# Four graph layers in one kernel: when statistics, a root, a short block, a weight product and a few copies are issued

## The chip, the cores and the metric

The kernel runs on one core of a Trainium2 chip. The metric is the device time of one execution in microseconds (us). The kernel before has a median of 2369.26 us over three runs (2368.26 to 2371.22).

A core has five engines with queues of their own, which run side by side and wait for each other by semaphores. The profile calls them PE (matrix products, into PSUM banks of 128 x 512 numbers), PEld (PE's weight load), DVE (element-wise work and statistics), ACT (copies, casts, exp, root), POOL (some element-wise work, and DMAs with computed addresses) and SP (which only issues DMAs).

## The reference, cut to what matters

A graph of 2708 nodes with 512 features passes four layers. Each ends in a layer norm of "x + layer(x)".

```python
deg = jnp.maximum((adj != 0).astype(jnp.float32).sum(-1), 1.0)
# layer 0: dinv = rsqrt(deg); relu(((dinv * (adj + I) * dinv) @ x + x) @ W + b)
x = _layernorm(x + _L0_gnn_ref(x, adj, deg[..., None], L0_gnn_W, L0_gnn_b), axis=-1)
# layer 1: dis = (deg + 1e-8) ** -0.5; ((dis * adj * dis) @ x) @ W.T + b
x = _layernorm(x + _L1_gnn_ref(x, adj, L1_gnn_W, L1_gnn_b), axis=-1)
# layer 2: two attention layers, each:
#   Wh, Ws = split(x @ W); a = softmax(Wh @ Ws.T) * adj; x = leaky_relu(a @ Wh + x)
x = _layernorm(x + _L2_gnn_ref(x, adj, L2_gnn_W_stack), axis=-1)
# layer 3: eight heads, which is adj @ (x @ W) + b
x = _layernorm(x + _L3_gnn_ref(x, adj, L3_gnn_W, L3_gnn_b), axis=-1)
```

The layer norm takes mean and variance over the 512 features of a node, with 1e-5 added to the variance ahead of the root.

## The kernel before, in words

**Tiling.** Nodes are cut into 22 blocks of 128 rows (`NB`), the last of which has only 20. As columns they form six chunks (`CH`): four of 512, one of 384, one of 276, that is of 4, 4, 4, 4, 3 and 3 blocks. As the summed dimension they form six row groups (`GROUPS`) of 4, 4, 4, 4, 3 and 3 blocks.

**Layers 0, 1 and 3** (class `Fast`). `step` goes through (layer, chunk, group). For a group, `prepare` casts adjacency bytes (tile `at`) to a factor `m` and splits the node rows into a high and a low part, `xh` and `xl`. `multiply` then adds `m` times both into the four banks of the chunk, tile `acc`. After the last group `evict` copies the sums into `ht`. While the next chunk is summed, `ends` finishes the one before: in phase 0 `project` multiplies by the weights (tile `mm`) and `combine` adds bias and residual for the first two blocks. In phase 1 the rest follow, and then `finish` calls `layernorm`, which does it for all blocks of the chunk: statistics (`st`, `mv`), the chain of small operations for the root (`rs_v`, `rs_t`, `rs_y`, `y`; one of them on ACT), and a pass per block that writes `o`. `combine` of the 20-row block first adds four partial products into `mm_sb` (`total`). During layer 1, `index` works out for attention which nodes each block takes from (tiles `up`, `rank`, `rest`, `both`, `list`). Its steps wait in a list of jobs and are handed out between the others.

**The two attention layers** (class `Attention`, layers 0 and 1 of their own). Scores of a chunk come from x times a mixed weight (`wst`, tile `mixed`, made by `mix`). For each of the 22 blocks, in the order `js`, `scores` does the products `sp` and ACT copies them to `s`; `greatest` keeps a running maximum (`top`). When the scores of the next chunk have begun, the old chunk's maximum is turned (`tr_top`, `mx`, `wide`, `tr_mx`: the functions `shift_rows` and `shift_columns`), `soften` makes exp and running sums (`sum`) for each block and writes weights to DRAM (`pairs`, by SP). Adjacency being sparse, `fetch` has POOL gather for each block only rows of nodes that occur (`g`). `weigh` multiplies these on PE into `acc`, and `end` scales, adds the residual, applies leaky ReLU, and in layer 1 calls the layer norm (tiles `xr`, `r`) at the chunk's last block.

**Overlap at the seams.** While the last chunk of attention's layer 0 is scored and softened, the generator `second` multiplies the weights of layer 1 (`mix(1)`) and projects. While the last chunk of its layer 1 is, `early` starts layer 3: groups 0 to 3 of its chunks 0, 1 and 2. As PSUM banks are few, the sums of these are copied to SBUF by ACT (tile `begun`) and added again in `evict`.

**What sets the order.** Each engine's instructions run in the order in which the program issues them: the class `Ordered` ties every instruction to the one before on its engine. This is why nearly all lines of the profile bear line 70, that of the helper, and are told apart by tile. Attention has a planner of its own: `advance(us)` moves an estimated clock on by what PE was given, `later(us, what)` puts work off until the clock has got there, and `advance` issues whatever has come due. `weigh` does a product only if the estimated landing of its rows has passed. `until(clock, fill)` takes rows or other layers' work until a time; the variable `done` in `layer` is such a time.

The lines that the change touches: `js` (1696) and `done` (1734) in `layer`, `mix` (1324 to 1346), the end of an attention block (1645 to 1671), `early` (626 to 630), `layernorm` (634), `combine` (976), and in `step` the call of `evict` (1073).

Of the kernel before, what the change touches and what calls it, by code (L numbers as in the profile page):

```python
# [19 lines left out]
P = 128  # L20
N = 2708
D = 512
# [469 lines left out]
class Layer:  # L492


    def __init__(self, number, source, weights, bias):
        self.number, self.source, self.weights, self.bias = number, source, weights, bias
        self.hi, self.lo = [None] * NB, [None] * NB
        self.rows = [None] * NB
        self.acc, self.ht, self.done, self.part = {}, {}, {}, {}
        self.begun = {}  # L500
        self.loaded = set()

# [11 lines left out]
class Fast:  # L514
# [17 lines left out]
    def run(self):  # L532
        kernel, nc = self.k, self.nc
        with ExitStack() as ctx:
            pool = lambda name, bufs, **kw: ctx.enter_context(
                self.tc.tile_pool(name=name, bufs=bufs, reuse_waits="tile", **kw)
            )
            self.pages, self.wides = pool("pages", PAGES), pool("wides", WIDES)
            self.small, self.lists = pool("small_f", 4), pool("lists", 1)
            self.banks = [pool(f"banks{h}", 4, space=PSUM) for h in range(2)]  # L540
            given = [kernel.x_in[bass.ts(i, P), :] for i in range(NB)]
            l0 = Layer(0, given, kernel.w0, kernel.b0)
            l1 = Layer(1, kernel.saved[0], kernel.w1, kernel.b1)
            l3 = Layer(3, kernel.saved[2], kernel.w3, kernel.b3)
            self.attention = attention = Attention(self)
            self.jobs, self.due, self.other, self.beats = [], None, 1, 0
            run = Run(l0, l1)
            for t in range(len(run.seq)):
                self.step(run, t)
            attention.project(attention.layers[0], 0)  # L550
            for g in range(3):
                self.ends(run, g)
                if g == 1:
                    attention.project(attention.layers[0], 1)


            run = Run(l3)
            run.seq = [(l3, k, g) for k in range(TWO) for g in range(4)]
            run.seq += [(l3, k, g) for g in (4, 5) for k in range(2)]
            run.seq += [(l3, k, g) for k in range(2, TWO) for g in (4, 5)]  # L560
            run.seq += [(l3, k, g) for k in range(TWO, len(CH)) for g in range(len(GROUPS))]
            attention.run(self.early(run))
            for j in range(*GROUPS[5]):
                l3.rows[j] = attention.made[j]
            for t in range(4 * TWO, len(run.seq)):
                self.step(run, t)

            ly, k = run.before
            for i, n, ps in self.project(ly, k):
                self.finish(ly, k, [(i, n, self.combine(ly, i, n, ps))])  # L570

    def work(self, engine):

# [24 lines left out]
    def early(self, run):  # L598

        seq = run.seq  # L600
        yield True
        self.load(*seq[0])
        self.load(*seq[1])
        yield True
        self.prepare(*seq[0])
        yield True
        for t in range(4 * TWO):
            ly, k, g = seq[t]
            if t < 2:
                self.attention.need(GROUPS[t + 2][1] - 1)  # L610
            self.load(*seq[t + 2])
            if t == 4:
                self.load_weights(ly)
            if t == 4 * TWO - 1:
                self.attention.need(GROUPS[4][1] - 1)
                for j in range(*GROUPS[4]):
                    ly.rows[j] = self.attention.made[j]
            self.prepare(*seq[t + 1])
            if g == 3:
                ly.begun[k] = []  # L620
            for n, j in enumerate(range(*GROUPS[g])):
                if t == 0:
                    self.multiply(ly, k, g, [j])
                else:
                    self.multiply(ly, k, g, ds=[n])
                self.attention.advance(2 * cost(CH[k][1]))
                if g == 3:
                    b = self.page(f"begun{k}_{n}")
                    self.nc.scalar.copy(b[:, : CH[k][1]], ly.acc[k][n][:, : CH[k][1]])
                    ly.begun[k].append(b)  # L630
                yield True


    def layernorm(self, rows):

        nc, small = self.nc, self.small
        m = len(rows)
        mv = small.tile([P, DC, 2], FP, tag="mv", name="mv")
        if any(n < P for _, _, n in rows):
            nc.vector.memset(mv, 1.0)  # L640
        for q, (r, _, n) in enumerate(rows):
            st = small.tile([P, 6], FP, tag="st", name="st")
            nc.vector.bn_stats(st[:n], r[:n])
            nc.vector.bn_aggr(mv[:n, q, :], st[:n])
        y = small.tile([P, DC], FP, tag="y", name="y")[:, :m]
        self.rsqrt(y, mv[:, :m, 1], LN_EPS)
        for q, (r, o, n) in enumerate(rows):
            nc.vector.tensor_scalar(
                o[:n], r[:n], mv[:n, q, 0:1], y[:n, q : q + 1], ALU.subtract, ALU.mult
            )  # L650
# [322 lines left out]
            x = ly.done["xres", i]  # L973
            self.nc.vector.tensor_add(x[:n], x[:n], ly.bt[:n])

    def combine(self, ly, i, n, ps):

        nc, x = self.nc, ly.done.pop(("xres", i))
        if n <= QW:
            t = self.page(f"mm_sb{ly.number}_{i}")  # L980
            self.total(t[:n], ps, n, D)
            ps = t
        if ly.number == 3:
            nc.vector.tensor_add(x[:n], x[:n], ps[:n])
            return x
        scale = (self.k.rdeg if ly.number == 0 else self.k.dis)[:n, i : i + 1]
        r = self.page(f"r{ly.number}_{i}")
        nc.vector.scalar_tensor_tensor(r[:n], ps[:n], scale, ly.bt[:n], ALU.mult, ALU.add)
        if ly.number == 0:
            nc.vector.scalar_tensor_tensor(x[:n], r[:n], 0.0, x[:n], ALU.max, ALU.add)  # L990
        else:
            nc.vector.tensor_add(x[:n], x[:n], r[:n])
        return x

    def finish(self, ly, k, parts):

        nc, out = self.nc, []
        for i, n, x in parts:
# [1 line left out]
            if n < P and ly.number == 0:  # L1000
                nc.vector.memset(o, 0.0)
            out.append((i, o, n))
        self.layernorm([(x, o, n) for (_, n, x), (_, o, _) in zip(parts, out)])
        for i, o, n in out:
            if ly.number == 3:
                nc.sync.dma_start(self.k.out[i * P : i * P + n, :], o[:n])
# [36 lines left out]
    def step(self, run, t):  # L1043
# [6 lines left out]
        if ly.number == 1 and k == len(CH) - 1 and g in (2, 3, 4):  # L1050
            self.attention.begin(g - 2)
        self.multiply(ly, k, g)
        wide = CH[k][1] == BANK
        if run.before and run.phase in ((1, 3, 4, 5) if wide else (1, 5)):
            self.work("PE")
# [9 lines left out]
        if g == len(GROUPS) - 1:  # L1065
# [4 lines left out]
            while run.before and run.phase < 2:  # L1070
                self.ends(run, run.phase)
                run.phase += 1
            self.evict(ly, k)
            run.before, run.phase = (ly, k), 0
            if ly.number == 1:
                self.jobs.append((k, self.index(k)))
# [2 lines left out]
    def ends(self, run, g):  # L1079
# [3 lines left out]
            run.parts = self.project(ly, k)  # L1083
            run.x = []
        if g in (0, 1):
            some = run.parts[:2] if g == 0 else run.parts[2:]
            run.x += [(i, n, self.combine(ly, i, n, ps)) for i, n, ps in some]
        if g == 1:
            run.o = self.finish(ly, k, run.x)
            if ly.number == 0 and k == len(CH) - 1:  # L1090
# [158 lines left out]
class Chunk:  # L1249


    def __init__(self, ly, k):
# [4 lines left out]
        self.softened = 0  # L1257
        self.fetched, self.rden = [], None
        self.x, self.first = {}, {}

        self.to_weigh = []
        for q, (i, _, _) in enumerate(self.blocks):
# [12 lines left out]
class Attention:  # L1275
# [48 lines left out]
    def mix(self, a):  # L1324
# [5 lines left out]
                nc.sync.dma_start(w[h][c], self.k.w2_t[a, h, bass.ts(c, P), :])  # L1330
        yield True
        ps = [self.bank(1 - a, f"mix{a}_{m}") for m in range(DC)]
        for c in range(DC):
            for m in range(DC):
                nc.tensor.matmul(
                    ps[m], w[1][c][:, bass.ts(m, P)], w[0][c], start=(c == 0), stop=(c == DC - 1)
                )
            self.advance(DC * cost(D))
            yield True
        for m in range(DC):  # L1340
            t = self.page(f"mixed{a}_{m}")
            nc.scalar.copy(t, ps[m])
            if a == 0:
                nc.sync.dma_start(self.mixed[m], t)
            else:
                self.layers[a].mixed.append(t)

    def load_w(self, ly):

# [295 lines left out]
    def end(self, ch, q, acc, x, first):  # L1645
# [3 lines left out]
        )  # L1649
        r = self.page(f"r2_{ch.name}_{q}")  # L1650
        if w < P:
            nc.vector.memset(r, 0.0)
        nc.vector.scalar_tensor_tensor(r[:w], x[:w], SLOPE, x[:w], ALU.mult, ALU.max)
        if ch.ly.number == 1:
            nc.vector.tensor_add(r[:w], r[:w], first[:w])
            ch.ends.append((r, w))
            if q == len(ch.blocks) - 1:
                self.f.layernorm([(r, r, w) for r, w in ch.ends])
                for (i, _, _), (r, _) in zip(ch.blocks, ch.ends):
                    nc.sync.dma_start(self.k.saved[2][i], r)  # L1660
                    self.made[i] = r
            return
        nc.sync.dma_start(self.k.between[i], r)
        ch.ends.append((r, w))
        if q == len(ch.blocks) - 1:
# [3 lines left out]
                    ch.ends, ch.k, 1, f"x2b{ch.k}", self.k.turned[1][ch.k], nc.sync  # L1669
                ),  # L1670
            )


    def run(self, next_layer):
# [15 lines left out]
    def layer(self, ly, chunks, fill):  # L1690
        f = self.f
        self.chunks, self.made = chunks, {}
        for k, ch in enumerate(chunks):
            old = chunks[k - 1] if k else None

            js = [0, 1, NB - 1, *range(2, NB - 1)]
            for n, j in enumerate(js):
                if old and n == 0:
                    self.load_masks(old)
# [31 lines left out]
        self.shift_rows(last)  # L1731
        self.until(self.clock + 3, fill)
        self.shift_columns(last)
        done = self.clock + 2
        while last.softened <= NB:
            self.soften(last)
            done += 1.4
# [106 lines left out]
```

## Time and profile before

| | |
|---|---|
| median of three runs | 2369.26 us |
| the profiled execution's own time | 2338.2 us |
| its span | 2336.5 us |
| mean granted clock of PE | 0.993 |
| PE busy | 2274.8 us, 97% |
| PEld busy | 1292.5 us, 55% |
| DVE busy | 1474.8 us, 63% |
| ACT busy | 662.2 us, 28% |
| POOL busy | 762.3 us, 33% |
| moved by DMA | 463.50 MB, 198 GB/s over the span |

All durations below come from the one profiled execution, whose span is inside its time. In a row of the timeline the columns are the start from the span's start, the duration, engine, line, operation, the written tile and the read ones, shape, count, and in brackets the engine's idle time just ahead and what released it. In the groups, "x" is a number of instructions. In the list of waits the columns are the waiting engine and tile, what ended the wait, the total, how often, and the longest. PE's idle time is what ties the other engines to the total; where another engine is idle, nothing follows from that alone.

### The profile page before, as it was taken

To read this page: it belongs to the slowest core of one execution; us is meant where nothing else is said; L and a number is where in the kernel's file an instruction comes from. 1 tells how busy PE (TensorE), PEld (TensorE's weight loads), DVE (VectorE), ACT (ScalarE), POOL (GpSimd) and SP (SyncE) were. 2 spreads that over 40 slices of the span, in tenths; PEclk is the share of its full clock that TensorE was granted. 3 is DMA by queue.
4 is the path that set the end of the run, shared out by engine and by line. 5 is a ranking of instruction groups with operands and counts; after the bars stand their busy time and mean duration, and the time that the engine had idled before them with its cause. 6 is when DMAs were issued, how large, how long until landed. Compare 5 with 4: busy or idle time off the path is not lost.

```text
span 2336.5 us, 26171 instructions
## 1 busy us (share of the span) xinstructions
PE 2274.8 (97%) x8518; PEld 1292.5 (55%) x8518; DVE 1474.8 (63%) x2831; ACT 662.2 (28%) x1334; POOL 762.3 (33%) x879
## 2 busy tenths in 40 slices
PE   8999999999999999999999999999999999999997
PEld 6677677778644444443456444444443456566585
DVE  6999986786655529657677511228677788724523
ACT  6544353223100113222223200113232334432211
POOL 6645641111000000636375550000636466551000
PEclk9999999999999999999999999999999999999998
DMA  9765652222434404869699996405869799983311
GB/s 343 258 199 169 182 172 86 74 86 70 171 146 167 154 0 143 278 229 311 204 324 350 302 388 232 152 0 163 279 217 314 233 316 329 305 279 96 123 48 43
DMA packets 312440, 463.50 MB, mean 198 GB/s; under 512 B 60162, under 2 KB 189706, under 8 KB 312292
## 3 DMA queue, kind: packets, MB, share of 16 engines
q1 hardware_dynamic: 252276, 240.81, 31.5%
q0 software_dynamic: 60016, 220.92, 27.1%
q8 instruction: 69, 1.13, 0.2%
q14 instruction: 79, 0.65, 0.1%
HBM read 307.75 MB, written 153.85 MB: 198 GB/s over the span
## 4 chain that ended last, share of the span: by engine, by line
PE 84%; DVE 7%; DMA 4%; issue 2%; ACT 1%; POOL 1%; SPq 0%; DVEq 0%; ACTq 0%; POOLq 0%
PE sp L70 32%; PE acc L70 29%; PE mm L70 9%; PE z L70 6%; PE wst L70 6%; DMA pairs<-s 1%; DMA at<-in_adj_t 1%; DVE st L70 1%; DMA at<-mask 1%; ACT m L70 1%; DVE s L70 1%; PE list L70 1%; PE mix L70 0%; POOL bytes L70 0%; PE tr_x2t L70 0%
## 5 line engine op out<-in xcount | busy, mean ns | idle before, releaser
L70 POOL DMA_INDIRECT g<-pairs,givers x510 | 516.2, 1012 | 897.0 <-DMA pairs<-s 537.4
L70 PE MATMUL sp<-xs,wst_sb 128*128 128x512 f32 (+3 forms) x2112 | 797.7, 544 | 0.0
L70 PEld LDWEIGHTS sp<-xs,wst_sb 128*128 128x128 f32 (+1 forms) x2112 | 380.0, 186 | 406.8 <-issue 321.9
L70 PE MATMUL acc<-m,xh 128*128 128x512 f32 (+4 forms) x1584 | 571.4, 382 | 13.6 <-ACT m L70 7.0
L70 PE MATMUL acc<-m,xl 128*128 128x512 f32 (+4 forms) x1584 | 553.2, 367 | 1.5 <-DVE xl L70 1.5
L70 PEld LDWEIGHTS acc<-m,xh 128*128 128x128 f32 (+1 forms) x1584 | 290.3, 189 | 81.4 <-issue 22.3
L70 PEld LDWEIGHTS acc<-m,xl 128*128 128x128 f32 (+1 forms) x1584 | 290.3, 189 | 48.1 <-issue 5.7
L70 ACT COPY s<-sp 128x512 f32<-128x512 f32 (+2 forms) x252 | 133.6, 531 | 482.1 <-PE sp L70 469.5
L70 PE MATMUL acc<-g 128*32 128x512 f32 (+1 forms) x1020 | 260.8, 605 | 0.9 <-DMA g<-pairs,givers 0.5
L70 DVE TENSOR_TENSOR top<-top,s 128x512 f32<-128x512 f32 (+5 forms) x240 | 149.6, 623 | 170.6 <-ACT s L70 169.1
L70 PE MATMUL mm<-w,ht 128*128 128x512 f32 (+1 forms) x528 | 222.6, 593 | 8.1 <-DVE ht L70 8.1
L70 ACT CAST m<-at 128x512 fp32r<-128x512 uint8 (+5 forms) x396 | 199.2, 567 | 80.0 <-DMA at<-mask 63.7
L70 ACT ACTIVATE s<-s 128x512 f32<-128x512 f32 (+3 forms) x264 | 150.7, 580 | 236.6 <-DVE s L70 236.3
L70 DVE TENSOR_TENSOR sum<-sum,s 128x512 f32<-128x512 f32 (+4 forms) x252 | 157.4, 625 | 23.9 <-ACT s L70 23.9
L70 DVE TENSOR_TENSOR s<-s,a 128x512 f32<-128x512 f32 (+3 forms) x264 | 165.9, 628 | 10.2 <-DMA a<-mask 1.2
L70 DVE TENSOR_TENSOR s<-s,shift 128x512 f32<-128x512 f32 (+3 forms) x264 | 162.8, 620 | 6.7 <-ACT shift L70 6.7
L70 PEld LDWEIGHTS mm<-w,ht 128*128 128x128 f32 (+1 forms) x528 | 95.5, 186 | 124.4 <-issue 110.9
L70 PE MATMUL wst<-xt,mixed 128*128 128x512 f32 (+2 forms) x384 | 152.5, 550 | 1.7 <-ACT mixed L70 1.7
L70 PEld LDWEIGHTS acc<-g 128*32 128x32 f32 (+1 forms) x1020 | 75.4, 134 | 136.9 <-issue 115.8
L70 PE MATMUL z<-w,xt 128*128 128x512 f32 (+1 forms) x352 | 151.0, 596 | 0.0
L70 DVE COPY z_sb<-z 128x512 f32<-128x512 f32 (+1 forms) x44 | 30.3, 690 | 179.5 <-PE z L70 176.3
L70 POOL DMA_DIRECT2D x<-o x44 | 26.0, 596 | 358.0 <-DVE o L70 354.2
(167 smaller groups left out, 1657.4 us busy)
## 6 DMA issues: line engine op xcount, KB each, us to landing
pairs<-s SPq DMA_DIRECT2D x378, 128.0 KB
pairs<-z_sb SPq DMA_DIRECT2D x84, 512.0 KB
at<-in_adj_t SPq DMA_DIRECT2D x84, 256.0 KB
xres<-x POOLq DMA_DIRECT2D x44, 256.0 KB, 4.3
x<-o POOLq DMA_DIRECT2D x43, 256.0 KB, 3.1
x<-x SPq DMA_DIRECT2D x37, 256.0 KB
at<-mask SPq DMA_DIRECT2D x32, 256.0 KB
xt<-t SPq DMA_DIRECT2D x32, 256.0 KB
```

The costliest lines, as they stand in the source:

```text
L70: ins = call(*args, **kw)
```

## The change

There are seven edits. First, `layernorm` is split into `means`, `statistics` and `normalize`. `combine` now calls `statistics` as soon as a block is combined, and `finish` calls `normalize` only; the same holds for an attention block's end. Second, in attention's layer 1 the root, the normalizing passes and the saves of a chunk are put off by two planner microseconds. Third, the 20-row block is scored fourth instead of third. Fourth, the weight product of attention's layer 1 is done output part by output part, with each part's copy right behind it. Fifth, in attention's layer 1 the time `done` starts at four instead of two planner microseconds. Sixth, the copies of begun sums are issued ahead of `advance`, and a memset moves from DVE to POOL. Seventh, for chunks with begun sums `evict` is called right after the last product, ahead of the phases of the chunk before.

```diff
@@ early
-                self.attention.advance(2 * cost(CH[k][1]))
                 if g == 3:
                     b = self.page(f"begun{k}_{n}")
                     self.nc.scalar.copy(b[:, : CH[k][1]], ly.acc[k][n][:, : CH[k][1]])
                     ly.begun[k].append(b)
+                self.attention.advance(2 * cost(CH[k][1]))
                 yield True
@@
-    def layernorm(self, rows):
+    def statistics(self, mv, q, r, n):
+        nc = self.nc
+        st = self.small.tile([P, 6], FP, tag="st", name="st")
+        nc.vector.bn_stats(st[:n], r[:n])
+        nc.vector.bn_aggr(mv[:n, q, :], st[:n])
+
+    def means(self, few):
+        mv = self.small.tile([P, DC, 2], FP, tag="mv", name="mv")
+        if few:
+            self.nc.vector.memset(mv, 1.0)
+        return mv
+
+    def normalize(self, mv, rows):
         nc, small = self.nc, self.small
         m = len(rows)
-        mv = small.tile([P, DC, 2], FP, tag="mv", name="mv")
-        if any(n < P for _, _, n in rows):
-            nc.vector.memset(mv, 1.0)
-        for q, (r, _, n) in enumerate(rows):
-            st = small.tile([P, 6], FP, tag="st", name="st")
-            nc.vector.bn_stats(st[:n], r[:n])
-            nc.vector.bn_aggr(mv[:n, q, :], st[:n])
         y = small.tile([P, DC], FP, tag="y", name="y")[:, :m]
@@
-    def combine(self, ly, i, n, ps):
+    def combine(self, ly, k, q, i, n, ps):
+        if q == 0:
+            ly.mv[k] = self.means(any(n < P for _, _, n in blocks_of(k)))
+        x = self.sum(ly, i, n, ps)
+        self.statistics(ly.mv[k], q, x, n)
+        return x
+
+    def sum(self, ly, i, n, ps):
         nc, x = self.nc, ly.done.pop(("xres", i))
@@ finish
-        self.layernorm([(x, o, n) for (_, n, x), (_, o, _) in zip(parts, out)])
+        self.normalize(ly.mv[k], [(x, o, n) for (_, n, x), (_, o, _) in zip(parts, out)])
@@ step
         self.multiply(ly, k, g)
+        if g == len(GROUPS) - 1 and k in ly.begun:
+            self.evict(ly, k)
...
-            self.evict(ly, k)
+            if k in ly.acc:
+                self.evict(ly, k)
@@ ends
-            some = run.parts[:2] if g == 0 else run.parts[2:]
-            run.x += [(i, n, self.combine(ly, i, n, ps)) for i, n, ps in some]
+            for i, n, ps in run.parts[:2] if g == 0 else run.parts[2:]:
+                run.x.append((i, n, self.combine(ly, k, len(run.x), i, n, ps)))
@@ mix
-        for c in range(DC):
-            for m in range(DC):
+        def end(m):
+            t = self.page(f"mixed{a}_{m}")
+            nc.scalar.copy(t, ps[m])
...
+        for e in range(DC):
+            for c, m in [(e, m) for m in range(DC)] if a == 0 else [(c, e) for c in range(DC)]:
                 nc.tensor.matmul(
                     ps[m], w[1][c][:, bass.ts(m, P)], w[0][c], start=(c == 0), stop=(c == DC - 1)
                 )
+            if a == 1:
+                end(e)
             self.advance(DC * cost(D))
             yield True
@@ end of an attention block
         if w < P:
-            nc.vector.memset(r, 0.0)
+            nc.gpsimd.memset(r, 0.0)
         nc.vector.scalar_tensor_tensor(r[:w], x[:w], SLOPE, x[:w], ALU.mult, ALU.max)
         if ch.ly.number == 1:
             nc.vector.tensor_add(r[:w], r[:w], first[:w])
+            if q == 0:
+                ch.mv = self.f.means(ch.cw % P)
+            self.f.statistics(ch.mv, q, r, w)
             ch.ends.append((r, w))
             if q == len(ch.blocks) - 1:
-                self.f.layernorm([(r, r, w) for r, w in ch.ends])
-                for (i, _, _), (r, _) in zip(ch.blocks, ch.ends):
-                    nc.sync.dma_start(self.k.saved[2][i], r)
-                    self.made[i] = r
+                self.later(2, lambda: self.normalize(ch))
             return
...
+    def normalize(self, ch):
+        self.f.normalize(ch.mv, [(r, r, w) for r, w in ch.ends])
+        for (i, _, _), (r, _) in zip(ch.blocks, ch.ends):
+            self.nc.sync.dma_start(self.k.saved[2][i], r)
+            self.made[i] = r
@@ layer
-            js = [0, 1, NB - 1, *range(2, NB - 1)]
+            js = [0, 1, 2, NB - 1, *range(3, NB - 1)]
...
-        done = self.clock + 2
+        done = self.clock + (2 if ly.number == 0 else 4)
```

## The prediction

> **What bounds the kernel.** I read the busy shares first, then the chain, and then TensorE's (PE's) waits, since the groups all carry one line, that of the ordering helper.
>
> The profile's busy row and its chain:
>
> ```profile
> span 2336.5 us, 26171 instructions
> ...
> PE 2274.8 (97%) x8518; PEld 1292.5 (55%) x8518; DVE 1474.8 (63%) x2831; ACT 662.2 (28%) x1334; POOL 762.3 (33%) x879
> ...
> PE 84%; DVE 7%; DMA 4%; issue 2%; ACT 1%; POOL 1%; SPq 0%; DVEq 0%; ACTq 0%; POOLq 0%
> ```
>
> PE is busy 97% of the span and holds 84% of the chain. The change leaves every matrix product in the program, so it can only take from what is left: 2336.5 - 2274.8 = 61.7 us of idle PE, and half-clock stretches. PE's last matmul ends some 17 us before the end, so about 45 us of idle lie inside. PE's waits, total, times and longest:
>
> ```profile
> engine line waited for: us in total, times, longest us
> PE mm L70 <- DVE ht L70: 8.1, 4, 2.6
> PE acc L70 <- ACT m L70: 7.0, 5, 2.9
> PE tr_mx L70 <- DVE wide L70: 4.5, 10, 0.7
> ...
> PE rest L70 <- DVE up L70: 4.1, 1, 4.1
> PE acc L70 <- DVE dg L70: 3.6, 1, 3.6
> PE acc L70 <- ACT begun L70: 2.9, 2, 2.7
> PE tr_top L70 <- DVE top L70: 1.9, 1, 1.9
> PE wst L70 <- ACT mixed L70: 1.7, 1, 1.7
> PE acc L70 <- DVE xl L70: 1.5, 2, 1.2
> ...
> PE acc L70 <- DMA g<-pairs,givers: 0.5, 2, 0.3
> ```
>
> Each part of the change moves work ahead of one of these. Costing it means asking, place by place, what the PE waits for next.
>
> A gap can cost more than itself. PE's timeline around the `begun` wait:
>
> ```profile
> 2119.46 0.39 PE L70 MATMUL acc<-m,xl 128*128 128x512 f32 x1
> 2122.55 0.80 PE L70 MATMUL acc<-m,xh 128*128 128x512 f32 x1 [2.70 <-ACT begun L70]
> 2123.14 0.63 PE L70 MATMUL acc<-m,xl 128*128 128x512 f32 x1
> 2123.57 0.63 PE L70 MATMUL acc<-m,xh 128*128 128x512 f32 x1
> ```
>
> The matmul takes 0.63 instead of 0.39 us, with starts 0.43 apart instead of 0.23; over 2120 to 2125 us the granted clock averages 0.76. Such a stretch is about 3.4 us at half clock and loses 1.7 us. It follows the gaps of 2.9 (ACT m, at 2012), 2.7 (begun), 3.6 (dg) and 4.1 us (rest), but neither the 2.6 us one at 2162 nor one of 2.67 us at 790.
>
> Here a rule is weighed. The Trainium skill, "TensorE: Matmul & The Clock Gate", Part 1, says that the clock halves after an idle window of about 3.4 us, a free-running one. By it a 2.7 us gap would usually cost 2.7 us, and a removal that leaves 1.9 us would bring 0.8. By the row it costs 4.4 and brings 2.5. The row decides where a gap is already there; for a new gap near 2.7 us I take half of the 1.7 us, since such gaps went either way here.
>
> **The change part by part** (us of PE time; the sum is made against the profiled execution's 2338.2 us).
>
> *Statistics per block.* The same instructions (0.66 + 0.18, about 0.8 a block) run as each block is combined, instead of all after the last. That pays where DVE otherwise waits for PE's next product and PE later waits for DVE. Around 652 DVE waits 1.96 us for `mm`; the first of three blocks' statistics fits there, so `up` and `rest` come 0.8 earlier: the gap of 4.1 becomes 3.3. Its half-clock stretch stays. In the same way the gap for `dg` at 309 loses some 0.5 (DVE waits 0.53 before), and the one for `xl` at 344 (1.2) some 0.8. In mid-chunks of layers 0 and 1 PE waits for nothing of this kind: nothing. That is covered by PE's own work; without cover it would cost at most 0.8 a block. The `list` waits (4.2 in all) hang on `both`, which follows PE's own `rest`: unchanged. At the very end blocks 19, 20 and 21 each get their own `memset` of 0.07: 0.15 lost. Sum: **2.1 - 0.15 = 1.95**.
>
> *The 20-row block fourth.* When a chunk's scores start, PE does three blocks and then the four small transposes `tr_mx` of the previous chunk, which need DVE's `wide`. The block just ahead of them is the 20-row one, x8 matmuls in 1.05 us; here at the fifth boundary of layer 0:
>
> ```profile
> 1224.18 0.49 PE L70 MATMUL tr_top<-ident,top 128*128 128x128 f32 x3
> 1224.60 0.66 PE L70 MATMUL sp<-xs,wst_sb 128*20 128x276 f32 x8
> 1226.00 0.52 PE L70 MATMUL tr_mx<-ident,wide 128*128 128x128 f32 x3 [0.74 <-DVE wide L70]
> ```
>
> With a full block there (1.9 us at 276 columns, 3.4 at 512, instead of 0.66 to 1.05), PE comes 1.2 to 2.4 us later and the 0.26 to 0.74 us waits are gone: layer 0 0.26+0.26+0.36+0.57+0.74 = 2.2, layer 1 0.35+0.35+0.36+0.56 = 1.6, **3.8**. Layer 1's last (0.74) is counted below. What goes the other way: the 20-row total (a copy and three adds on DVE, 0.67 + 3 x 0.7 = 2.8 us) now lies after softening has begun, so softening, pair writes (SP) and fetches (POOL) of the old chunk move 2 to 4 us later against PE. Their cover is the 12 to 16 us between a chunk's first fetched rows landing and PE's use of them; without it every us late is a PE us.
>
> *Root put off (attention's layer 1).* The root's chain and the four saves on SP go two planner-us later: on ACT behind the exp of block 20 and a score copy, on SP behind the pair writes of block 19. In mid-chunks the saves are wanted far later: nothing. At 1919 it matters. DVE's root chain there (rs_v 1915.6, four normalizing passes to 1919.1, two `top`) is what `tr_top` waits 1.86 us for. Moved, ACT does the score copy of block 20 first (ends 1915.95), then the table load of 1.28, then the root (1917.4); normalizing ends near 1920.5 instead of 1919.1, `top` twice makes `tr_top` about 1921.8: a gap of 2.7. The 0.74 wait for `tr_mx` goes: 1.86 + 0.74 = 2.6 against 2.7, plus half of 1.7 for the clock: **-1.0** (bounds: +0.5 if the earlier statistics let the whole root start first, -2.5 with the full half-clock stretch and some lateness).
>
> *W2 product by parts.* The PE order is turned round so that output part e is done after four matmuls, and ACT copies it while PE does the next. Before, ACT's four copies (2.03 us) started only at 1304.10:
>
> ```profile
> 1303.76 0.43 ACT L70 ACTIVATE s<-s 128x276 f32<-128x276 f32 x1 [0.76 <-DVE s L70]
> 1304.10 2.03 ACT L70 COPY mixed<-mix 128x512 f32<-128x512 f32 x4
> ```
>
> and `wst` waited for the first. Now only the last part's copy is left at that point, and `wst` needs it at its fourth matmul, 2.6 us in. The copies are ahead of softening's exps on ACT, which come up to 2.2 us later and then have 2 us fewer ahead of them. **1.7**.
>
> *Order after attention's last chunk* (`done` 4 instead of 2 in layer 1). It puts fetched-row products of chunk 4 ahead of layer 3's second row group, so more PE work covers DVE's and ACT's preparation of `m` and `xh`. The waits for `m` at 2012 (2.9 + 0.31 + 0.30), 0.3 nearby, and 1.7 of half clock, some 5.5 in all, go. But the fetched rows are now the late ones: POOL issues one every 1.25 us and each lands some 6 us later, so the six come from 1996.4 to 2003.1, and PE would stand before them for some 4.0 in small waits. **1.5** (bounds -1 to +4; the middle, by the fetch rows of this same stage). DMA is the limit here: its share over 1985 to 2005 is 1.06, over 1965 to 1985 1.04.
>
> *Copies of begun sums ahead of the planner's step.* ACT's copy of the chunk's fourth sum stood behind an `rs_t` that waited for DVE:
>
> ```profile
> 2121.82 0.20 ACT L70 ACTIVATE rs_t<-rs_v 128x3 f32<-128x3 f32 x1 [6.53 <-DVE rs_v L70]
> 2121.93 0.57 ACT L70 COPY begun<-acc 128x512 f32<-128x512 f32 x1
> ```
>
> Now the copy comes first, and the 2.70 gap and its half clock (1.7) go. Next late is the mask page of group 5, queued on SP behind the three saves of that root: it lands about 2127, its fold, high part and `m` take to about 2131, and PE waits some 1.9 there. The `memset` of the last block's result moves to POOL (0.5 less on DVE). 4.4 - 1.9 = **2.5** (bounds 0, if the mask page is later by 2.5; 4.4, if it isn't late).
>
> *Sums of the last chunks taken in early.* For chunks 0 to 2 of layer 3 the four adds into `ht` (0.68 each) are issued ahead of the previous chunk's combination and statistics, so the 2.62 wait at 2162 goes, with 0.27 of slow first matmul. The profile shows DVE at normalizing work just there, from 2156.7 to 2164.1. The statistics and outputs behind them are wanted by nobody on PE. The next sums' banks come free just in time, I allow 0.2. **2.7**.
>
> **Sum:** 1.95 + 3.8 - 1.0 + 1.7 + 1.5 + 2.5 + 2.7 = 13.15 us. The runs shown have a median of 2369.26, 31 above the profiled one; nothing moved here lies in that difference, so I take the same 13.2 us off: **2356 us** (-0.56%). A measurement of this kernel tells 0.2% (4.7 us) from no change.
>
> **The rivals.**
> 1. *As summed*, 0.65: 2350 to 2359, with the unknown terms at their bounds.
> 2. *The end of attention keeps its time*, 0.16. The stage from 1985 to 2165 is bound by fetches and mask pages, and what the last three parts free is waited for at the next page. For it: DMA 0.94 busy over 1985 to 2075. Against: DMA falls to 0.44 by 2115 to 2130, and at 2162 no transfer is named. It leaves 1.95 + 3.8 - 1.0 + 1.7 = 6.5: 2363.
> 3. *The score reordering doesn't do what it says*, 0.12: `wide` is late again behind the moved 20-row total, as DVE is 78% busy over 1568 to 1925, and rival 2 holds too. Against: the total comes after the transposes' inputs in DVE's order. It leaves under 3: 2367, no change to be told.
> 4. *Slower*, 0.07: later softening makes the fetched rows late at ten chunk boundaries. It decides above 13.2 / 10 = 1.3 us per boundary, and shows as slower above 1.8. For it: POOL's fetches wait mostly for pair writes (537 us in the profile's groups), and in the last chunk DVE is 98% busy (19.55 of 20 us, 1945 to 1965). Against: PE waited for fetched rows 0.5 us in the whole run. At 2.5 us each: 2369 - 13 + 25 = 2381.
>
> **How the numbers follow.** The forecast is rival 1's. Faster: 0.65 and nearly all of rival 2, 0.80; same: rival 3 and the rest of 2, 0.13; slower 0.07. The range 2348 to 2366 holds rivals 1 and 2 but for 1's low tail, and part of 3; it leaves out the slower case and about 0.1 besides.
>
> **What would show it.** Right: in the profile after, PE's waits of `tr_mx` for `wide`, of `wst` for `mixed`, of `acc` for `begun` and of `mm` for `ht` near 2162 are missing; `rest` for `up` is near 3.3; PE busy is less only by half-clock time (some 3 us). Also a `tr_top` wait near 2.7, several small `acc` waits for `g` near the last chunk's start, and one of `acc` for `m` of about 2 near group 5. Wrong: `g` waits at each chunk boundary (rival 4), `tr_mx` waits still there (3), or waits for `at` and `g` summing to more than 6 us after 1985 (2).

## The result, and the profile after

The changed kernel has a median of 2357.37 us over seven runs (2350.50 to 2359.66), the kernel before 2368.33 over seven. The ratio is 0.9946, with a 95% interval from 0.9927 to 0.9966: 0.54% faster, where 0.56% was forecast. The total is met. How it comes about is not what was forecast, as the experiments show: the term for the statistics is several times too small, the four edits at the end of attention (root put off, `done`, begun copies, early `evict`) together lose time instead of gaining it, and on one chip the same change gained only a quarter of the sum.

The first profiles can't be laid side by side. That of before took 2338.2 us, 30 less than its own median; that of the changed kernel took 2359.7. The experiments suggest why: the same program has a median of 2341 us on one chip and of 2366 to 2368 on two others. The chips of the first two profiles are not on record. So below, an execution is compared only with one on the same chip.

The busy row of the changed kernel, and PE's waits in it (columns as before):

```profile
span 2357.8 us, 26154 instructions
...
PE 2283.9 (97%) x8518; PEld 1296.6 (55%) x8518; DVE 1478.0 (63%) x2831; ACT 662.4 (28%) x1334; POOL 767.3 (33%) x881
```

```profile
PE acc L70 <- ACT m L70: 8.6, 5, 3.8
PE tr_mx L70 <- DVE wide L70: 6.2, 2, 3.6
PE acc L70 <- ACT begun L70: 5.8, 1, 5.8
PE mm L70 <- DVE ht L70: 5.3, 3, 2.4
...
PE tr_mx L70 <- ACT x2b L70: 3.4, 1, 3.4
...
PE tr_top L70 <- remote: 2.6, 1, 2.6
```

Two lines of before are gone, as forecast: `wst` for `mixed`, and the ten short waits of `tr_mx`. One is there that was not forecast: a wait of 5.8 us for `begun`, twice as long as the one that the change was to remove.

### The profile page after: what moved, and what is told of

It reads as the page before. It is cut to its first block, busy times and chain, and to the rows that moved or that the text cites. A ratio compares the mean times of both kernels' runs of the same rounds, so it can differ in the third digit from the quotient of the medians.

```text
span 2357.8 us, 26154 instructions
## 1 busy us (share of the span) xinstructions
PE 2283.9 (97%) x8518; PEld 1296.6 (55%) x8518; DVE 1478.0 (63%) x2831; ACT 662.4 (28%) x1334; POOL 767.3 (33%) x881
## 3 DMA queue, kind: packets, MB, share of 16 engines
q1 hardware_dynamic: 252276, 240.81, 31.3%
## 5 line engine op out<-in xcount | busy, mean ns | idle before, releaser
L70 DVE TENSOR_TENSOR top<-top,s 128x512 f32<-128x512 f32 (+2 forms) x240 | 149.1, 621 | 150.3 <-ACT s L70 108.9
```

The lines of the kernel that those rows point to most:

```text
L70: ins = call(*args, **kw)
```

## The experiments

Three groups of four kernels, each group on one chip beside the kernel before. The medians are over 5 to 21 runs, those of before over 11 to 51. The ratios are to that kernel, with 95% intervals; they are not always the quotient of the two medians.

| group (median of before) | kernel | median, us | ratio |
|---|---|---|---|
| 1 (2341.21) | before again | 2342.07 | 1.0003 [0.9989, 1.0017] |
| 1 | changed again | 2337.91 | 0.9986 [0.9977, 0.9994] |
| 1 | changed, 20-row block third | 2340.65 | 0.9998 [0.9989, 1.0006] |
| 1 | changed, four end edits undone | 2328.71 | 0.9937 [0.9916, 0.9958] |
| 2 (2366.16) | changed, `done` at 2 | 2355.09 | 0.9950 [0.9933, 0.9968] |
| 2 | changed, root not put off | 2349.39 | 0.9925 [0.9902, 0.9948] |
| 2 | changed, begun copies behind `advance` | 2354.60 | 0.9948 [0.9932, 0.9964] |
| 2 | changed, late `evict` | 2352.93 | 0.9938 [0.9922, 0.9955] |
| 3 (2367.61) | before with the statistics alone | 2356.91 | 0.9959 [0.9943, 0.9976] |
| 3 | changed again | 2354.86 | 0.9949 [0.9931, 0.9967] |
| 3 | changed, four end edits undone | 2346.89 | 0.9920 [0.9899, 0.9940] |
| 3 | before again | 2368.43 | 1.0002 [0.9986, 1.0018] |

### Both kernels once more

No edit.

> The kernel before once more, unchanged: 0% by definition. Two readings of the gap of 30 us between the first profiled execution (2338.2) and the median of its runs (2369.3). Reading 1, that execution was an unusually quick one: this profile lies near 2368 and its PE waits hold some 25 to 30 us more, at places where the changed kernel's profile has them too (DVE and ACT late behind transfers at the ends of attention's layers). Reading 2, profiled executions are quicker: again near 2338 with the same waits.

> The changed kernel once more, unchanged. My sum gives -13 us against the kernel before (ratio 0.9945). If the sum's rows hold, the four waits named in the prediction (wst for mixed, mm for ht near 2162, the short tr_mx waits at chunk boundaries, begun behind rs_t) are missing in this execution too, while the waits of 2.6 to 5.8 us for late transfers in the first profile of it (at 1230, 1930, 1935, 2006, 2052, 2156) change place or size. If those are made by the change itself, they stand at the same places with the same sizes.

Reading 1 of the profile of before is out in this form: here the runs themselves were at 2342, as the first profile had been, and the waits were nearly those of it. The changed kernel gained only 0.14% on this chip (0.06 to 0.23%), some 3 us, where 13.2 were forecast. PE's waits in its profile, span 2333.9 us:

```profile
PE acc L70 <- ACT m L70: 7.9, 6, 3.5
PE acc L70 <- ACT begun L70: 6.3, 1, 6.3
PE mm L70 <- DVE ht L70: 5.9, 3, 2.4
...
PE rest L70 <- DVE up L70: 3.5, 1, 3.5
PE tr_top L70 <- DVE top L70: 2.6, 1, 2.6
PE acc L70 <- DVE dg L70: 2.1, 1, 2.1
PE tr_mx L70 <- DVE wide L70: 1.9, 1, 1.9
PE acc L70 <- DMA g<-pairs,givers: 1.5, 5, 0.5
```

`tr_top` waits 2.6 and fetched rows are waited for five times, as forecast. Of the waits of the first profile that nobody forecast, those near 1230 (3.4) and 1935 (2.6) are not here and the one near 2006 (3.6) is 1.9, so they vary from chip to chip or execution to execution. The one for `begun` is here and in every execution of the changed kernel, so it is the change's own. The one for `m` at group 5 was forecast, at 1.9; it is 3.8 in the first profile and 3.5 here.

To see where time is gained and lost, take the start of the same matmul in the two timelines of group 1, before and changed, from front to back: `rest` 669.3 and 665.4; first `tr_top` of attention 872.9 and 870.6; first `wst` of attention's layer 1 1308.7 and 1300.1; its last `tr_top` 1989.2 and 1977.7; first `mm` of layer 3 2147.0 and 2143.3; PE's last 2325.8 and 2317.6. The gain reaches 11.5 us, falls to 3.7 over the end of attention, and grows to 8.3 behind it (this execution of before was 2 us above its median, and the changed one 2 below). With the four end edits undone the same points of the last three are 1980.6, 2135.8 and 2310.6: gains of 8.6, 11.2 and 15.2. Behind that last `tr_top`, the kernel without the edits gains another 6.6 us on the kernel before, and the one with them loses 3.2. The edits, which were to save 5.7 us, cost 9.8 there.

### The four end edits undone

```diff
-                self.later(2, lambda: self.normalize(ch))
+                self.normalize(ch)
...
-        done = self.clock + (2 if ly.number == 0 else 4)
+        done = self.clock + 2
...
-        if g == len(GROUPS) - 1 and k in ly.begun:
-            self.evict(ly, k)
...
+                self.attention.advance(2 * cost(CH[k][1]))
                 if g == 3:
                     b = self.page(f"begun{k}_{n}")
                     self.nc.scalar.copy(b[:, : CH[k][1]], ly.acc[k][n][:, : CH[k][1]])
                     ly.begun[k].append(b)
-                self.attention.advance(2 * cost(CH[k][1]))
```

> The changed kernel with the four edits at attention's end undone (root put off, done at 4, begun copies first, early evict). My sum: these are worth -1.0 + 1.5 + 2.5 + 2.7 = 5.7 us, so this lies 5.7 above the changed kernel and 7.5 below the one before (ratio 0.997). Rival: the end of attention is bound by fetches and mask pages and the four edits bring nothing: ratio near 0.9945, as the changed kernel.

> The changed kernel without the four end edits once more: as where it was measured first, 5 to 9 us quicker than the changed one beside it (ratio to before near 0.993), with no begun wait above 1 us. Rival: the 9 us were that occasion's; then both are the same.

Neither my sum nor its rival: the kernel was 9.2 us quicker than the changed one in group 1, and 8.0 in group 3, by the medians. In group 1 the intervals lie apart; in group 3 they overlap a little. It beats both kernels on both occasions. PE's waits of it in group 1:

```profile
PE mm L70 <- DVE ht L70: 5.3, 4, 2.4
...
PE acc L70 <- ACT begun L70: 0.8, 1, 0.8
PE tr_top L70 <- DVE top L70: 0.7, 1, 0.7
```

Without the end edits, the waits that these were to remove have shrunk all the same: `begun` 2.7 to 0.8, `tr_top` 1.9 to 0.7, and `mm` for `ht` near 2162 (2.6) is 0.3. The statistics per block, which this kernel keeps, are the likely cause; below they are run alone.

The largest wait that the edits brought in their place is seen around 2022. First the timelines of PE, ACT and SP in the changed kernel:

```profile
2022.48 0.39 PE L70 MATMUL acc<-m,xl 128*128 128x512 f32 x1
2029.16 0.79 PE L70 MATMUL acc<-m,xh 128*128 128x512 f32 x1 [6.29 <-ACT begun L70]
2029.75 0.63 PE L70 MATMUL acc<-m,xl 128*128 128x512 f32 x1
```

```profile
2026.45 2.18 ACT L70 CAST m<-at 128x512 fp32r<-128x512 uint8 x4 [5.19 <-DMA at<-mask]
2028.53 0.57 ACT L70 COPY begun<-acc 128x512 f32<-128x512 f32 x1
```

```profile
2011.24 11.39 SPq L70 DMA_DIRECT2D pairs<-s  x24
2022.68 0.49 SPq L70 DMA_DIRECT2D at<-mask  x1
```

And ACT and SP with the four edits undone:

```profile
2021.08 2.18 ACT L70 CAST m<-at 128x512 fp32r<-128x512 uint8 x4 [1.10 <-DMA at<-mask]
2023.17 0.58 ACT L70 COPY begun<-acc 128x512 f32<-128x512 f32 x1
```

```profile
2008.18 9.84 SPq L70 DMA_DIRECT2D pairs<-s  x21
2018.12 0.38 SPq L70 DMA_DIRECT2D at<-mask  x1
```

On ACT the begun copy stands behind four casts, which wait for a mask page. SP issues that page behind pair writes, three for each block that softening has finished: 24 of them in the changed kernel, 21 without the edits. The page goes out at 2022.68 instead of 2018.12, the copy ends at 2029.1 instead of 2023.8, and the bank that PE wants next is free only then. PE then runs 6.8 us at half clock (0.76 granted on the mean of 2022 to 2036).

Not all of this is loss. Without the edits PE stands a little earlier, and has its half clock there (0.76 over 2008 to 2022, where the changed kernel has 1.00):

```profile
2011.11 0.50 PE L70 MATMUL acc<-m,xh 128*128 128x512 f32 x1 [3.12 <-ACT m L70]
```

So the waits behind the last `tr_top` have to be set against each other. With half-clock losses they sum to 19.0 us in the changed kernel and 8.8 without the edits. The difference of 10.2 is: `begun` 5.5 more; `m` at group 5 2.7 more, and 1.7 for the half clock behind it; `tr_mx` 1.9 more; fetched rows 1.3 more; `m` near 2011 2.6 less, and 0.3 less for `mm`. The half clock at `begun` and that at 2011 cancel.

### The four, one at a time

Each kernel has one of the four pieces of the diff above undone.

> The changed kernel with the root of attention's layer 1 not put off. The recorded step gives the putting off -1.0 us: tr_top's wait falls from 2.6 back to 0.7, as it is without all four end edits (the earlier statistics alone shorten it from 1.9), and the kernel is 1.9 us quicker than the changed one, or 3.6 with a half-clock stretch less. Rival for the 9 us that the four edits cost: the saves and the pair writes change their order on SP, so that mask pages come late; then the wait of 6.3 us for begun goes in this run.

> The changed kernel with done at 2 again in attention's layer 1, the other three end edits kept. New theory after the run without all four: done at 4 lets PE run through the row groups of layer 3 in one stretch (1998.7 to 2022.9), so that it stands before the begun copy, which lies behind casts that wait for a mask page: 6.3 us, and 1.7 of half clock. Then this kernel has no wait of acc for begun above 1 us and is 5 to 8 us quicker than the changed one (ratio to before near 0.996 here). My recorded step has it the other way: 1.5 us slower than the changed kernel.

> The changed kernel with the begun copies behind the planner's step again. PE's order is the same. The recorded step says 2.5 us slower (the wait of 2.7 us at 2120 comes back). If the earlier statistics have already taken most of that wait (0.8 left of 2.7 in the run without the four edits), it is 1 us slower or no different. If the copies' new place makes the wait of 6.3 us at 2029, that wait goes and the kernel is 8 us quicker.

> The changed kernel with the sums of the last layer's first chunks taken in as late as before. The recorded step says 2.7 us slower (mm waits 2.6 for ht near 2162). But without all four end edits that wait is missing too: if the statistics per block alone remove it, no difference (within 0.5 us).

Putting off the root is what makes the wait for `begun`. Of the executions profiled, the seven with the root put off all wait for `begun` around 2030 to 2050: 5.8, 6.3, 6.2 and 8.2 us in the changed kernel and the one with the short block third, 4.7, 6.3 and 3.9 with `done`, the copies and `evict` undone. The three without (this one and twice all four undone) have no such wait there, and none for `begun` above 0.8 anywhere. With the root alone undone, the page stands in SP's order two blocks' writes earlier, 18 of them just ahead of it instead of 24:

```profile
2027.33 8.40 SPq L70 DMA_DIRECT2D pairs<-s  x18
2035.83 0.38 SPq L70 DMA_DIRECT2D at<-mask  x1
```

With `done` at 2 it is 27 with the root put off and 21 without: both times putting off the root adds the writes of two blocks. The kernel's ratio is 0.9925, against 0.9946 and 0.9949 of the changed kernel where that stood beside a kernel before of the same speed: some 5 us, though the intervals overlap. By these numbers the root accounts for about half of what the four edits cost. The wait for `m` at group 5 stays in each of these four kernels (2.5 to 3.9 us), and is 0.8 or less with all four undone: no single undoing removes it, and its cause stays open. My theory for `done` fell: with it undone the wait stayed (4.7), and the time is that of the changed kernel. For the copies and `evict` the times, good to some 4 us, can't tell; the profiles can. With the copies in their old place no begun wait is left near 2150, and with the late `evict` the `mm` wait near 2188 is 0.27 us. Both edits aim at a wait of which the statistics had left little.

### The statistics alone

The kernel before, with `combine` and attention's `end` calling `statistics`, and nothing else.

> The kernel before with the statistics per block alone. The recorded step gives 2 us. New theory, from the runs with the end edits undone: the statistics alone remove what I had put down to the end edits: the mm wait for ht near 2162 (2.6), most of the begun wait (2.7 to 0.8, with its 1.7 of half clock), most of tr_top's wait (1.9 to 0.7), besides rest 4.1 to 3.5 and dg 3.2 to 2: together some 10 us, but 2 to 3 of it go into a wait for m at group 5. So 7 to 8 us below the kernel before (ratio 0.9968), and the ten tr_mx waits (4.5) stay.

0.9959 [0.9943, 0.9976] or 9.7 us, with bounds of 5.7 and 13.5: the 7 to 8 expected lie inside, the 2.0 of the step on record does not. Three of its waits from the end of attention on, in PE's timeline:

```profile
1934.91 0.52 PE L70 MATMUL tr_top<-ident,top 128*128 128x128 f32 x3 [0.60 <-DVE top L70]
...
2151.08 0.50 PE L70 MATMUL acc<-m,xh 128*128 128x512 f32 x1 [1.23 <-ACT begun L70]
...
2190.01 2.41 PE L70 MATMUL mm<-w,ht 128*128 128x512 f32 x5 [0.28 <-DVE ht L70]
```

And in the kernel before on the same chip:

```profile
1937.33 0.52 PE L70 MATMUL tr_top<-ident,top 128*128 128x128 f32 x3 [1.75 <-DVE top L70]
...
2149.25 0.50 PE L70 MATMUL acc<-m,xh 128*128 128x512 f32 x1 [2.71 <-ACT begun L70]
...
2190.68 1.55 PE L70 MATMUL mm<-w,ht 128*128 128x512 f32 x3 [2.62 <-DVE ht L70]
```

Besides, `dg` falls from 3.6 to 2.5 and `rest` from 4.1 to 3.5. That is 6.6 us together. The profiled execution itself was the slowest of this kernel's eleven (2363.2) and has other waits besides, among them one of 3.3 for another `begun` copy at 2102, so the 9.7 can't be summed from it. The `m` wait of 2 to 3 us that was expected at group 5 is 0.6.

### The short block third again

```diff
-            js = [0, 1, 2, NB - 1, *range(3, NB - 1)]
+            js = [0, 1, NB - 1, *range(2, NB - 1)]
```

> The changed kernel with the 20-row block third again. My sum: the ten short tr_mx waits come back, +3.8 us (ratio to before near 0.996). Rival: the waits of 3.4 us at 1230 and 2.6 us at 1935 come from the new order, as a full block's copy now needs a page that a transfer still holds; then they go, and this kernel is 2 us quicker than the changed one (ratio near 0.9935).

It was 2.7 us slower than the changed kernel by the medians (the intervals overlap), and its ten waits are back:

```profile
PE tr_mx L70 <- DVE wide L70: 4.7, 10, 0.7
```

The changed kernel has one such wait of 1.9 instead: 4.7 - 1.9 = 2.8. The rival's waits for `x2b` do not occur on this chip. On the others the changed kernel has them (2.5 us in group 3, 3.4 in the first profile), but on the third chip the kernel before waits near 1230 as well, and longer:

### The kernel before on the third chip

No edit.

> The kernel before, profiled beside these. If its time here is near 2366 as in the second group of runs, its profile has waits that the first one (2338) lacks, at 1230 and after 1980 and by DVE and ACT for transfers; if near 2341, it has the same waits as the first.

Its time was 2368.43, and its profile (span 2362.4) has the extra waits. Near 1230, on PE, DVE and ACT:

```profile
1233.80 0.87 PE L70 MATMUL tr_mx<-ident,wide 128*128 128x128 f32 x3 [6.38 <-DVE wide L70]
```

```profile
1232.51 0.56 DVE L70 TENSOR_REDUCE mx<-tr_top 128x3 f32<-128x384 f32 x1 [8.62 <-remote]
```

```profile
1231.08 0.39 ACT L70 COPY s<-sp 128x276 f32<-128x276 f32 x1 [6.01 <-remote]
```

DVE stands for 8.6 us although its operand was there 5.7 us earlier (`tr_top` ended at 1226.8), and ACT for 6.0; "remote" means that the profile shows no releaser. All PE waits sum to 63.2 us in this profile and to 47.8 in that of before on the first chip, and half clock costs 18.8 and 15.4: that is 18.8 of the 20 us between the two spans.

## Why the prediction was right, and where it was wrong

The sum was 13.2 us, and 11 came, but this agreement is in good part luck, in two ways.

The first is the chip. The sum was made on a profile of 2338 us, and carried over to a median of 2369 because "nothing moved here lies in that difference". That step was wrong. On the chip where the kernel before takes 2341 us, and shows nearly the waits that were costed, the change gained some 3 us; the 11 to 13 came where the kernel before takes 2367 to 2368. Why the gain differs stays open.

The second is the terms. By the medians of group 3 the steps from before to changed are: statistics 10.7 (9.7 by the ratio) instead of 2.0; the reordering, the W2 product and the moved `memset` together 10.0 instead of 5.5; the four end edits 8.0 lost instead of 5.7 gained. They make 12.7. Each step is good to some 4 to 6 us, so the 10.0 is not clear of 5.5, but the first and the last are clear of their forecasts: one error too low and one too high, and they largely cancel.

**Statistics per block**: the step's mechanism held where it was applied. `rest` went from 4.1 to 3.5 (forecast 3.3). In the changed kernel the wait for `xl` near 344 fell from 1.2 to 0.5 in two executions of three (forecast 0.4) and the one for `dg` by 1.0 to 1.4 (forecast 0.5); three variants with the same statistics keep 1.2 to 1.3 for `xl`. It failed in its extent: it was costed for layers 0 and 1 only. The waits at the end of attention hang on a layer norm just the same, and I put them down to the edits that name them. These were costed as if the statistics still stood where they were.

**The 20-row block fourth**: right in mechanism, as the ten waits go and come back with it. 3.8 was forecast and 2.7 measured on the first chip. The difference between the waits there is one new wait of 1.9 at the last chunk; it is missing with the four end edits undone, so it isn't shown to be the reordering's.

**Root put off**: `tr_top`'s new wait was forecast at 2.7 and measured 2.6, and of the seven executions with the root put off five had a half-clock stretch behind it, where half was allowed. The step that failed is its price, -1.0. It moved the saves on SP and looked no further down that queue than the pair writes. A mask page behind the pair writes went one or two blocks later, with ACT's casts, the begun copy behind these and a PSUM bank hanging on it: a wait of 6.3 us that the sum does not have. What the root costs on the whole is some 5 us, by its single undoing.

**W2 product by parts**: the wait is gone in all profiles of the changed kernel, so 1.7 or, on the first chip, 3.9 (before again) is right. It isn't safe: with the end edits undone the same edit left 3.4 in one execution. There the last part's copy stood on ACT behind an exp, and the exp's input on DVE behind a product that waited for a mask:

```profile
1303.37 0.45 DVE L70 TENSOR_TENSOR s<-s,a 128x276 f32<-128x276 f32 x1 [12.00 <-DMA a<-mask]
```

```profile
1304.21 0.43 ACT L70 ACTIVATE s<-s 128x276 f32<-128x276 f32 x1 [9.12 <-DVE s L70]
1304.55 0.57 ACT L70 COPY mixed<-mix 128x512 f32<-128x512 f32 x1
```

```profile
1305.17 3.59 PE L70 MATMUL wst<-xt,mixed 128*128 128x512 f32 x4 [3.35 <-ACT mixed L70]
```

**Order after the last chunk, copies of begun sums, early sums**: 1.5 + 2.5 + 2.7 was forecast; undoing any one of them made no loss that the times can tell. `done` did what it was to do at its own place: the waits for `m` near 2011 are 0.9 in the changed kernel of group 1 and 3.6 without the edits, and fetched rows cost 1.3 there where 4.0 was allowed. But PE only came earlier to the `begun` wait. The wait that was expected to come next, for `m` at group 5, was 3.5 in the changed kernel (forecast 1.9), with a half-clock stretch behind it that wasn't costed, and 0.8 without the edits. The 0.15 us at the very end did not show: from the start of PE's last matmul to the end of the span it is 16.4 us in both kernels of group 1.

Rival 2, that the end of attention is bound by fetches and pages, was nearest to what happened there. It underrated it: the time freed was not just waited for at the next page, a later page made the waits longer. Its sign on record, waits for `at` and `g` of more than 6 us after 1985, is met if the `begun` wait of 6.3 is counted to the mask page that it hangs on. That the half-clock stretches would come and go held: the same wait of 2.7 us for `list` near 790 was followed by one in the changed kernel and not in the kernel before, in group 1. The Trainium skill's "free-running" window ("TensorE: Matmul & The Clock Gate", Part 1) agrees with that; its idle window of 3.4 us as a threshold doesn't, as gaps of 2.3 to 2.9 us also had one; here the measurement decides.

## What to carry to other kernels

When several edits aim at waits that hang on one chain, cost the earliest edit on all of them first, and the others only on what it leaves. For a step put off, walk every in-order queue that it is moved past to the first transfer behind it that another engine waits for: here the writes of two blocks ahead of one page cost some 5 us. A wait that an edit removes or makes counts only against the waits that take its place. A right total proves nothing about the terms; undoing parts in groups on one chip found a version 8 to 9 us quicker than the change.

## What the runs showed of the hardware

The same program is 1.1% slower on two chips (2366 and 2368 us) than on a third (2341), and the gain of the change differs as well: 0.14% on that one, 0.51% on the third and 0.54% in the first measurement. Each chip was used on one occasion, so chip and hour are not told apart. Busy times and DMA traffic are alike: in the two profiles of before, on the first and third chip, the hardware queue takes 31.5% and 31.3% of the DMA engines, the software queue 27.0% and 27.2%. The slower one has stalls of 4 to 9 us on DVE and ACT in attention, at 1002, 1102 and 1231 among others, for which no releaser is shown and which the quicker one lacks. The DMA engines are 1.00 to 1.04 busy around these three, but in the quicker one as well (1.01 to 1.04), so their load alone does not tell the two apart. What holds the engines there stays open.

A half-clock stretch lasted 3.4 us in most cases, and 6.8 behind the wait of 6.3 us for `begun`.
